# A two-layer graph kernel on one core: tile lists and row ranks moved to the head of the dense stage

## The chip, the cores and the metric

The kernel runs on one core of a Trainium2 chip. The metric is the time on the device in microseconds; the kernel before takes 857.63 us, the median of three runs (855.54 to 860.32). Its profile was taken from one further execution with a span of 857.5 us.

## The reference

There are 8 batches of 2048 nodes with 128 features, and one 2048 x 2048 matrix `adj`, which is sparse: about 0.4% of it is nonzero, and it is weighted.

```python
def layer0(x):                            # relation = adj
    w_j, w_i, w_r = g_w[:128], g_w[128:256], g_w[256]
    res = (x @ w_i)[:, :, None] + (x @ w_j)[:, None, :] + adj[None] * w_r + g_b
    return einsum('bij,bjd->bid', res, x) @ weight + bias

def layer1(x):                            # A1 = A2 = adj
    x1 = einsum('bnf,nw->bwf', x, adj)
    x2 = 2 * einsum('bnf,nw->bwf', x1, adj) - x
    xs = [x, x1, x2, x1, x2]
    return relu(concat(xs) @ Theta1 + bias1)

x = layernorm(x + layer0(x))
x = layernorm(x + layer1(x))
```

Layer 0 is the product of adj (with the weights folded in, y0 = x @ (w_r * weight)) and a term of rank 9, whose rows are in the tile `ub`. Layer 1 is, after some algebra, two hops: two products with the transpose of adj.

## The kernel before, in words

The 2048 nodes are cut into 16 chunks of 128 (NC). A chunk of outputs of layer 0 could be computed as 16 products of a 128 x 128 block of adj (transposed) with a chunk of y0, for all batches, and the kernel does so for three chunks only (ND = 3), those with 0 to 2. For the other 13 it uses the sparsity of adj: for each tile of 32 output columns it has a list of up to 128 rows that have an entry in that tile, gathers those rows of y0 from memory, gathers the matching rows of adj (called R), and multiplies. Rows that don't fit the lists of the 32-column tiles go into lists of the 64-column halves, and then into one list for the chunk of 128. So a chunk has 4 + 2 + 1 = 7 gathers of y0 and 7 of R. The same lists serve all products with adj.

The stages, in order:

1. *Load* (until about 144 us). `mask_rows` and `y_chunk` (lines 297 and 323) load adj and x, transpose them on the PE, find which tiles have entries on DVE, compute y0 into `Y[c]` (all 16 chunks stay in SBUF), and add up the first dense chunk. The transposed adj goes into the table of R, `rr_d[c]`, one for each sparse chunk: its row n holds the 128 entries of adj to chunk c transposed, and then the 128 entries not transposed. `copy_r` (L410) fills the second half from adj, with one DMA of 1 MB per chunk, in 512-byte pieces. The last 9 rows of each table hold the coefficients of the rank-9 term; they come from the small stores at the end of `more_rows` (L589 to L602, DMA at L599).
2. *Dense stage* (the loop at L798, about 144 to 262 us). Three rounds, c = 0 to 2. Round c ends dense chunk c (`rank1` adds the rank-9 term, `finish0` adds x and does the layernorm), and adds up dense chunk c + 1 in 16 steps j of two 128 x 128 x 512 matmuls (L846). Between these steps the list work is written out by hand: this is where the change is.
3. *Sparse stage of layer 0* (about 258 to 440 us). For each of the 13 chunks in the order `seq` (9 to 14, 3 to 8, 15), `listed_rows` multiplies gathered rows (L881), `finish0` and `make_u` end the chunk. The gathered rows of y0 go to nine buffers, `Y[0]` to `Y[8]`, which the dense stage must have read.
4. *Two hops* of layer 1, with gathers from `u_d` and `y_d` (to the end).

The list work of the dense stage has these parts. `tile_ranks` (L482) counts, with a matmul, the rank of each row in its tile, and keeps 8 rows of each row chunk. `tile_lists` (L496) transposes the result on the PE and sorts each piece with MAX8 on DVE. `tile_lists_end` (L627) turns it into the indices of the tile lists. `half_ranks` and `chunk_ranks` (L528, L541) count the ranks of what is left, by `ranks` (L510): a running sum over the 16 row chunks, with one matmul per row chunk that adds its sums to all later ones. `candidates` (L550) transposes the rest, `list_round` (L558) takes the 8 largest of 2048 per list with MAX8 and strikes them out with MATCH_REPLACE, eight times over, and `chunk_lists_end` (L630) makes the last indices.

`gathers` (L696) issues gathers of R from a fixed list of jobs, `sets` (L686): (c, True) are the four tile lists of a chunk, (c, False) its two half lists and the chunk list. They go to four buffers (`stages`); `keep_r` (L668) copies a landed set under a mask to its place, on DVE. With `mm` given, a gather waits for that matmul ("pace"). In the sparse stage `put` issues what is missing for a chunk before it is used. All gathers are issued by GpSimd (POOL), each in turn (L646). Plain loads, copies and stores around here are issued by SyncE (SP), in the order of the program; a queued store that must wait holds all that follow it. The `pt` PSUM tiles have two buffers, so a tile waits for the last but one to be read.

Where the dense matmuls of round c = 1 meet the list work, one line sets the order: the matmul at j = 8 is placed behind the small matmul at the end of the lists.

Of the kernel before, what the change touches and what calls it, by code (L numbers as in the profile page):

```python
# [18 lines left out]
def kernel(  # L19
# [89 lines left out]
    def flat(t):  # L109
        return t.rearrange("p b f -> p (b f)")  # L110
# [299 lines left out]
    def copy_r(n0, n1):  # L410
        for c in seq[n0:n1]:
            tc.keep_in_program_order(
                nc.sync.dma_start(out=rr_d[c - ND][0:N, 1, :], in_=adj[:, c * P:(c + 1) * P])
            )
# [67 lines left out]
    def tile_ranks():  # L482

        for g in range(2):
            pr = p_tr.tile([P, NC // 2, NT], F32, name=f"pr{g}", tag="pt")
            cs = slice(g * NC // 2, (g + 1) * NC // 2)
            tc.keep_in_program_order(
                nc.tensor.matmul(pr, ut, one[:, cs, :], start=True, stop=True)
            )
            nc.vector.scalar_tensor_tensor(  # L490
                onen[:, cs, :], pr, 8.0, onen[:, cs, :], op0=ALU.is_le, op1=ALU.mult
            )
        nc.vector.tensor_add(hit, pairs(onen)[:, :, :, 0], pairs(onen)[:, :, :, 1])
        nc.vector.scalar_tensor_tensor(half, hit, 0.0, half, op0=ALU.is_equal, op1=ALU.mult)
# [14 lines left out]

    def ranks(out, m):  # L510

        tc.keep_in_program_order(
            nc.tensor.matmul(out, lt, m, start=True, stop=False, skip_group_check=True)
        )
        for c in range(NC - 1):
            tc.keep_in_program_order(nc.tensor.matmul(
                out[:, c + 1:, :], ones,
                m[:, c, None, :].to_broadcast([P, NC - 1 - c, m.shape[2]]),
                start=False, stop=(c == NC - 2), skip_group_check=True,
            ))  # L520

    def split(rank, m, mn, lo, hi, most):

# [34 lines left out]
    def list_round(r):  # L558
        top = lists[0:96, 64 + 8 * r:72 + 8 * r]
        part = cand[0:96].rearrange("p c n -> p (c n)")  # L560
        tc.keep_in_program_order(nc.vector.max(top, part))
        if r < 7:
            nc.vector.match_replace(part, top, part, 0.0)
# [6 lines left out]
    def make_ub():  # L570
        lq3 = lq.rearrange("p (b m) -> p b m", b=B)
        cs4 = rows4("cs4")
        for h in range(2):
            nc.scalar.copy(cs4[:, h * HB:(h + 1) * HB, :], pcs[h])
        pcq = p_tr.tile([P, B, 2], F32, name="pcq", tag="pt")
        for b in range(B):
            nc.tensor.matmul(
                pcq[:, b, :], cs4[:, b, :], sel[:, 0:2 + b % HB:1 + b % HB], start=True, stop=True
            )
        nc.vector.tensor_copy(lq[:, 0:(B - 1) * (B + 2) + 1:B + 2], pcq[:, :, 0])  # L580
        nc.vector.tensor_copy(lq3[:, :, B], pcq[:, :, 1])
        for h in range(2):
            pu = p_sm.tile([B + 1, HB, D], F32, name=f"pu{h}", tag="sm")
            for i in range(HB):
                nc.tensor.matmul(pu[:, i, :], lq3[:, h * HB + i, :], w_sb, start=True, stop=False)
                nc.tensor.matmul(pu[:, i, :], e8, b0row, start=False, stop=True)
            nc.vector.tensor_copy(ub[:, h * HB:(h + 1) * HB, :], pu)

    def more_rows():  # L589

        tc.keep_in_program_order(nc.sync.dma_start(out=y0_d[N:, :], in_=flat(ub)))
        n = (NC - ND) * (B + 1)
        ps = p_tr.tile([P, P], F32, name="ps", tag="pt")
        nc.tensor.transpose(ps[0:n, :], si[:, ND:, :].rearrange("p c b -> p (c b)"), ident)
        t = rows4("sit_all")
        nc.vector.memset(t[:, 1, :], 0.0)
        nc.scalar.copy(t[0:n, 0, :], ps[0:n, :])
        for c in seq:
            tc.keep_in_program_order(nc.sync.dma_start(  # L599
                out=rr_d[c - ND][N:, :, :],  # L600
                in_=t[(B + 1) * (c - ND):(B + 1) * (c - ND + 1), 0:2, :],
            ))  # L602
# [24 lines left out]
    def tile_lists_end():  # L627
        return lists_end(0, LP, [(h, 0, lists[:, 0:64], 64 * h, NT) for h in range(2)])
# [167 lines left out]
    with nc.allow_non_contiguous_dma(reason="512-byte rows of blocks"):  # L796
        pending, accs, xr = None, acc0, load_x(0, "xr", nc.sync)
        for c in range(ND):  # L798
            if c + 1 < ND:
                xr1 = load_x(c + 1, "xr", nc.sync)  # L800
            if c == 0:
                copy_r(2, NC - ND)
                tile_ranks()
                make_ub()
                more_rows()
                rank1(0, accs, si_t(0))
            else:
                z = finish0(c, accs, xr, c > 1)
            if c == 1:
                for n in range(NC):  # L810
                    tc.keep_in_program_order(
                        nc.sync.dma_start(out=y0_d[n * P:(n + 1) * P, :], in_=flat(Y[n]))
                    )
            if c + 1 < ND:
                accs1, sit, at1 = acc_pair(), si_t(c + 1), first_at[c + 1]
                for j in range(NC):
                    if c == 0:
                        if j == 0:
                            tile_lists()
                            z = finish0(c, accs, xr, False)  # L820
                        if j == 3:
                            at = tile_lists_end()
                            half_ranks()
                        if j == 6:
                            chunk_ranks()
                        if j in (8, 9):
                            candidates(2 * j - 16)
                            candidates(2 * j - 15)
                        if j == 10 or j == 13:
                            list_round(j // 13)  # L830
                        if j == 11:
                            layernorm(z, "0_0", at)
                    else:
                        if j < 8 and j % 3 < 2:
                            list_round(2 + j // 3 * 2 + j % 3)
                        if j == 8:
                            made, at = chunk_lists_end()
                            layernorm(z, "0_1", at)
                            fetch_own(0, y0_d, seq[0])
                            late0 = fetch_block(0, seq[0])  # L840
                    if (c > 0 or j > 3) and not (c == 1 and j > 12):
                        gathers(3 if c == 1 and j == 12 else 1 if j % 4 == 3 else 2, mm)
                    if c == 1 and j > 12:
                        fetch_lists(0, y0_d, seq[0], 2 * j - 24)
                    for h in range(2):
                        mm = nc.tensor.matmul(  # L846
                            accs1[h], at1[:, j, :], Y[j][:, h * HB:(h + 1) * HB, :],
                            start=(j == 0), stop=False, skip_group_check=True,
                        )
# [228 lines left out]
```

## Time and profile before

| | PE | DVE | ACT | POOL |
|---|---|---|---|---|
| busy us of 857.5 | 757.0 | 363.6 | 173.7 | 427.3 |
| share | 88% | 42% | 20% | 50% |

| costliest groups | count | busy us | mean ns |
|---|---|---|---|
| gathers from y0 and y, POOL L646 | 203 | 201.4 | 992 |
| gathers of R, POOL L646 | 91 | 92.3 | 1014 |
| gathers from u, POOL L646 | 112 | 111.1 | 992 |
| matmuls of listed rows, PE L881, into rc | 896 | 219.8 | 605 |
| matmuls of the dense stage, PE L846 | 128 | 61.5 | 633 |

In all, the DMA engines move 269.19 MB. A line "PE MATMUL acc<-Y,wide 128*128 128x512" is a matmul from tile Y with weights from tile wide; each matmul in float32 leaves two records. DMA_INDIRECT is a gather; "rr_d" is the table of R, "in_adj_dram" the matrix, "y_d" stands for y0_d in stage 3 and for y_d later. Times are from the start of the span. A busy PE is not a PE at its peak, and idle time of an engine off the chain of waits costs nothing.

### The profile page before, as it was taken

The page shows a single profiled execution, that of the slowest core. Times are in us where ns is not written, and L with a number is a line of the kernel's source. Part 1 is how long each engine was busy: PE and PEld are TensorE (multiplying, and loading weights), DVE is VectorE, ACT ScalarE, POOL GpSimd, SP SyncE. Part 2 cuts the span into 40 slices and gives each one's busy share as a digit, 9 for nine tenths or more (in the row PEclk, how much of TensorE's full clock was granted, in tenths as well). Part 3 has the DMA queues.
Part 4 walks back from the last instruction along what each step waited for, and adds up shares of the span by engine and source line. Part 5 has one row for each costly group of instructions (what it writes and reads, how often), then busy time and mean ns, then how long its engine had stood idle before and what let it go on. Part 6 is the DMA issues. An engine that isn't in the chain of part 4 may idle for free.

```text
span 857.5 us, 10765 instructions
## 1 busy us (share of the span) xinstructions
PE 757.0 (88%) x3594; PEld 377.8 (44%) x3594; DVE 363.6 (42%) x1060; ACT 173.7 (20%) x428; POOL 427.3 (50%) x438
## 2 busy tenths in 40 slices
PE   5999999999468898889997998899999999999993
PEld 4666665464134443434344443343433354544441
DVE  5555667344963453535453010000100075665664
ACT  3665664010002121212222000000000011111111
POOL 0000000007767777777764567766565556666660
PEclk9999999699869999999998999999999999999998
DMA  8699998998728999999996899999997899999994
GB/s 288 197 308 309 309 308 237 301 271 341 269 73 297 329 364 340 343 338 378 369 391 213 291 357 357 369 369 371 385 378 273 312 341 356 351 335 337 326 339 136
DMA packets 177548, 269.19 MB, mean 314 GB/s; under 512 B 17698, under 2 KB 127701, under 8 KB 175438
## 3 DMA queue, kind: packets, MB, share of 16 engines
q0 software_dynamic: 50400, 151.21, 48.7%
q1 hardware_dynamic: 103900, 90.02, 32.7%
q10 hardware_dynamic: 23186, 27.20, 8.7%
q8 instruction: 30, 0.49, 0.2%
q14 instruction: 32, 0.26, 0.1%
HBM read 246.75 MB, written 62.55 MB: 361 GB/s over the span
## 4 chain that ended last, share of the span: by engine, by line
DMA 39%; PE 21%; issue 7%; POOL 3%; DVE 1%; POOLq 0%; ACT 0%; DVEq 0%
DMA Y<-y_d,idx 22%; DMA Y<-u_d,idx 15%; PE acc L881 12%; PE acc L865 4%; PE acc L939 3%; POOL Y L646 2%; DMA stage<-rr_d,idx 2%; POOL stage L646 1%; PE pt_p L184 1%; PE pt_r L957 1%; PE pp L402 1%; DMA rd<-in_adj_dram 1%; POOLq L646 0%; DVE st L211 0%; DVE z L229 0%
## 5 line engine op out<-in xcount | busy, mean ns | idle before, releaser
L646 POOL DMA_INDIRECT Y<-y_d,idx x203 | 201.4, 992 | 105.7 <-PE acc L881 53.7
L881 PE MATMUL acc<-Y,rc 128*32 128x512 f32 (+2 forms) x896 | 219.8, 605 | 24.5 <-DMA Y<-u_d,idx 14.3
L646 POOL DMA_INDIRECT stage<-rr_d,idx x91 | 92.3, 1014 | 225.5 <-PE pc L554 190.5
L646 POOL DMA_INDIRECT Y<-u_d,idx x112 | 111.1, 992 | 64.5 <-PE acc L881 35.4
L881 PEld LDWEIGHTS acc<-Y,rc 128*32 128x32 f32 (+2 forms) x896 | 58.6, 128 | 175.4 <-issue 83.7
L881 PE MATMUL acc<-Y,rct 128*32 128x512 f32 (+2 forms) x364 | 108.6, 618 | 17.0 <-DMA Y<-y_d,idx 16.2
L865 PE MATMUL acc<-Y,rd 128*128 128x512 f32 x148 | 70.7, 601 | 4.1 <-DMA rd<-rr_d 4.1
L881 PEld LDWEIGHTS acc<-Y,rct 128*32 128x32 f32 (+2 forms) x364 | 26.3, 128 | 89.3 <-issue 44.4
L846 PE MATMUL acc<-Y,wide 128*128 128x512 f32 x128 | 61.5, 633 | 0.0
L219 ACT ACTIVATE st<-st,epst 128x8 f32<-128x8 f32 x32 | 9.9, 310 | 243.3 <-DVE st L218 243.3
L383 DVE TENSOR_TENSOR xs<-acc,xs 128x512 f32<-128x512 f32 x26 | 17.7, 682 | 93.5 <-PE acc L881 77.7
L176 DVE COPY z<-acc 128x512 f32<-128x512 f32 x9 | 6.2, 692 | 110.2 <-PE acc L881 57.9
L184 PE MATMUL pt_a<-ident,rc 128*128 128x128 f32 x256 | 38.3, 285 | 6.5 <-DMA rc<-in_adj_dram 6.0
L958 DVE TENSOR_TENSOR z<-acc,b1bc 128x512 f32<-128x512 f32 x32 | 21.5, 685 | 42.8 <-PE acc L865 27.6
L332 PE MATMUL acc<-wx,tr_x 128*128 128x130 f32 x256 | 36.5, 286 | 3.5 <-ACT tr_x L178 3.1
L311 DVE TENSOR_REDUCE stage<-rct 128x64 f32<-128x2048 f32 x13 | 29.7, 2286 | 23.0 <-ACT rct L178 23.0
L303 DVE TENSOR_REDUCE rc<-rc 128x64 f32<-128x2048 f32 x16 | 36.5, 2279 | 5.8 <-DMA rc<-in_adj_dram 5.8
L332 PEld LDWEIGHTS acc<-wx,tr_x 128*128 128x128 f32 x256 | 32.8, 194 | 13.8 <-ACT tr_x L178 6.2
L184 PEld LDWEIGHTS pt_a<-ident,rc 128*128 128x128 f32 x256 | 31.4, 147 | 16.3 <-issue 14.8
L342 PE MATMUL acc<-Y,wide 128*128 128x512 f32 x64 | 36.4, 652 | 1.7 <-ACT Y L336 0.9
L846 PEld LDWEIGHTS acc<-Y,wide 128*128 128x128 f32 x128 | 25.0, 203 | 29.0 <-issue 28.1
L959 DVE SCALAR_TENSOR_TENSOR z<-z,pt_r 128x512 f32<-128x512 f32 x32 | 20.5, 682 | 37.9 <-PE pt_r L957 37.9
(216 smaller groups left out, 897.3 us busy)
## 6 DMA issues: line engine op xcount, KB each, us to landing
rc<-in_adj_dram SPq DMA_DIRECT2D x16, 1024.0 KB
rr_d<-rct SPq DMA_DIRECT2D x13, 1024.0 KB
rr_d<-in_adj_dram SPq DMA_DIRECT2D x13, 1024.0 KB
xs<-in_x_dram SPq DMA_DIRECT2D x21, 512.0 KB
y_d<-Y SPq DMA_DIRECT2D x16, 512.0 KB
out_dram<-z ACTq DMA_DIRECT2D x16, 512.0 KB
u_d<-u ACTq DMA_DIRECT2D x15, 512.0 KB
Y<-y_d SPq DMA_DIRECT2D x15, 512.0 KB
```

Source lines behind the costliest of these rows:

```text
L184: mm = nc.tensor.transpose(pt[:, i, :], s, ident)
L303: nc.vector.tensor_reduce(mk[:, c, :], a.rearrange("p (w f) -> p w f", f=TW), AX.X, ALU.max, apply_absolute_value=True,)
L311: nc.vector.tensor_reduce(mkt[:, :, 4 * c:4 * c + 4], at.rearrange("p j (t f) -> p j t f", f=TW), AX.X, ALU.max, apply_absolute_value=True,)
L332: nc.tensor.matmul(py[:, i, 0:D + 2], xt[b // HB][:, (b + i) % HB, :], wx, start=True, stop=True,)
L342: nc.tensor.matmul(acc0[h], first_at[0][:, c, :], Y[c][:, h * HB:(h + 1) * HB, :], start=(c == 0), stop=False, skip_group_check=True,)
L646: g = nc.gpsimd.indirect_dma_start(out=out, out_offset=None, in_=src, in_offset=bass.IndirectOffsetOnAxis(ap=ids[:, n:n + 1], axis=0), bou ...
L846: mm = nc.tensor.matmul(accs1[h], at1[:, j, :], Y[j][:, h * HB:(h + 1) * HB, :], start=(j == 0), stop=False, skip_group_check=True,)
L865: in_order(nc.tensor.matmul(accs[h], r, t[:, h * HB:(h + 1) * HB, :], start=start, stop=stop, skip_group_check=True,))
L881: in_order(nc.tensor.matmul(accs[h][w * t:w * t + w], r[:, o + w * t:o + w * t + w], gs[t][:, h * HB * D:(h + 1) * HB * D], start=False, s ...
L939: in_order(nc.tensor.matmul(accs[h][:, b, :], x1t[c][:, h * HB + b, :], th[:, i, :], start=(b == 0), stop=False, skip_group_check=True,))
L958: nc.vector.tensor_add(z[:, hs, :], accs[h], b1bc.to_broadcast([P, HB, D]))
L959: nc.vector.scalar_tensor_tensor(z[:, hs, :], z[:, hs, :], 0.0, pt, op0=ALU.max, op1=ALU.add)
```

## The change

The list work is moved to the head of the dense stage, and three things go with it.

- *Order.* The tile lists, half ranks and chunk ranks come before round 0's last step, rather than at j = 0, 3 and 6; candidates at j = 0 and 1 rather than 8 and 9; six list rounds in round 0 (at every second step from 5) rather than two; the end of the lists at j = 7 of round 1 rather than 8.
- *Ranks by groups.* `ranks` sums groups of four row chunks on DVE (`four`). Within a group it adds each chunk to the later ones of the group with three matmuls over all groups at once, and then each group's sum to all later groups, with three more. It is seven matmuls for sixteen.
- *Stores.* The small stores for the table of R stand behind two copies of adj (four with the two before them), not behind all; the other nine copies follow them. The store of `ub` to y0_d moves to round 1. In `make_ub` the row b0row is added by one matmul for four batches.
- *Gathers.* Two gathers of R are issued at every step of round 0 from the first on, three at its end, and 23 in round 1: 58 in the dense stage, where it was 47. The list of jobs has all tile lists but the last at its front.

```diff
     def ranks(out, m):
-        tc.keep_in_program_order(
-            nc.tensor.matmul(out, lt, m, start=True, stop=False, skip_group_check=True)
-        )
-        for c in range(NC - 1):
-            tc.keep_in_program_order(nc.tensor.matmul(
-                out[:, c + 1:, :], ones,
-                m[:, c, None, :].to_broadcast([P, NC - 1 - c, m.shape[2]]),
-                start=False, stop=(c == NC - 2), skip_group_check=True,
-            ))
+        w = m.shape[2]
+        four = two.rearrange("p c w -> p (c w)")[:, 0:NG * w].rearrange("p (g w) -> p g w", w=w)
+        o4, m4 = [t.rearrange("p (g k) w -> p g k w", k=4) for t in (out, m)]
+        nc.vector.tensor_reduce(four, m.rearrange("p (g k) w -> p g w k", k=4), AX.X, ALU.add)
+        add(out, lt, m, start=True, stop=False)
+        for k in range(3):
+            add(o4[:, :, k + 1:, :], ones,
+                m4[:, :, k:k + 1, :].to_broadcast([P, NG, 3 - k, w]), start=False, stop=False)
+        for g in range(NG - 1):
+            add(out[:, 4 * g + 4:, :], ones,
+                four[:, g:g + 1, :].to_broadcast([P, NC - 4 - 4 * g, w]),
+                start=False, stop=(g == NG - 2))
...
             pu = p_sm.tile([B + 1, HB, D], F32, name=f"pu{h}", tag="sm")
+            nc.tensor.matmul(
+                pu, e8, b0row[:, None, :].to_broadcast([1, HB, D]), start=True, stop=False,
+                skip_group_check=True,
+            )
             for i in range(HB):
-                nc.tensor.matmul(pu[:, i, :], lq3[:, h * HB + i, :], w_sb, start=True, stop=False)
-                nc.tensor.matmul(pu[:, i, :], e8, b0row, start=False, stop=True)
+                nc.tensor.matmul(
+                    pu[:, i, :], lq3[:, h * HB + i, :], w_sb, start=False, stop=(i == HB - 1),
+                    skip_group_check=True,
+                )
...
     def more_rows():
-        tc.keep_in_program_order(nc.sync.dma_start(out=y0_d[N:, :], in_=flat(ub)))
...
-    sets = [(c, True) for c in seq[:10]]
+    sets = [(c, True) for c in seq[:-1]]
     for n, c in enumerate(seq):
         sets.append((c, False))
-        if n in (0, 4, 7):
-            sets.append((seq[10 + (0, 4, 7).index(n)], True))
+        if n == 4:
+            sets.append((LAST, True))
...
             if c == 0:
-                copy_r(2, NC - ND)
+                copy_r(2, 4)
                 tile_ranks()
+                tile_lists()
+                half_ranks()
                 make_ub()
                 more_rows()
+                copy_r(4, NC - ND)
+                at = tile_lists_end()
+                chunk_ranks()
                 rank1(0, accs, si_t(0))
+                mm = None
             else:
                 z = finish0(c, accs, xr, c > 1)
             if c == 1:
+                tc.keep_in_program_order(nc.sync.dma_start(out=y0_d[N:, :], in_=flat(ub)))
                 for n in range(NC):
...
                     if c == 0:
-                        if j == 0:
-                            tile_lists()
+                        if j < 2:
+                            candidates(2 * j)
+                            candidates(2 * j + 1)
+                        if j == 2:
                             z = finish0(c, accs, xr, False)
-                        if j == 3:
-                            at = tile_lists_end()
-                            half_ranks()
-                        if j == 6:
-                            chunk_ranks()
-                        if j in (8, 9):
-                            candidates(2 * j - 16)
-                            candidates(2 * j - 15)
-                        if j == 10 or j == 13:
-                            list_round(j // 13)
-                        if j == 11:
                             layernorm(z, "0_0", at)
+                        if j > 4 and j % 2:
+                            list_round((j - 5) // 2)
                     else:
-                        if j < 8 and j % 3 < 2:
-                            list_round(2 + j // 3 * 2 + j % 3)
-                        if j == 8:
+                        if j in (1, 3):
+                            list_round((j + 11) // 2)
+                        if j == 7:
                             made, at = chunk_lists_end()
                             layernorm(z, "0_1", at)
                             fetch_own(0, y0_d, seq[0])
                             late0 = fetch_block(0, seq[0])
-                    if (c > 0 or j > 3) and not (c == 1 and j > 12):
-                        gathers(3 if c == 1 and j == 12 else 1 if j % 4 == 3 else 2, mm)
-                    if c == 1 and j > 12:
-                        fetch_lists(0, y0_d, seq[0], 2 * j - 24)
+                    if c == 0:
+                        gathers(2, mm)
+                    elif j < 11:
+                        gathers(3 if j in (7, 8) else 1 if j == 3 else 2, mm)
+                    else:
+                        fetch_lists(0, y0_d, seq[0], 2 * j - 20)
...
-                        if c == 1 and j == 8:
+                        if c == 1 and j == 7:
                             behind(mm, made)
                 rank1(c + 1, accs1, sit)
                 if c == 0:
-                    gathers(2, mm)
+                    gathers(3, mm)
```

More of the change, by code (lines that the diff above doesn't have):

```diff
@@ L510, in ranks, with add @@
     def ranks(out, m):
-        tc.keep_in_program_order(
-            nc.tensor.matmul(out, lt, m, start=True, stop=False, skip_group_check=True)
-        )
-        for c in range(NC - 1):
-            tc.keep_in_program_order(nc.tensor.matmul(
-                out[:, c + 1:, :], ones,
-                m[:, c, None, :].to_broadcast([P, NC - 1 - c, m.shape[2]]),
-                start=False, stop=(c == NC - 2), skip_group_check=True,
-            ))
+        def add(o, wt, mv, **flags):
+            tc.keep_in_program_order(
+                nc.tensor.matmul(o, wt, mv, skip_group_check=True, **flags)
+            )
[11 more added lines that the diff above has]
+                start=False, stop=(g == NG - 2))
     def split(rank, m, mn, lo, hi, most):
@@ L583, in make_ub @@
             pu = p_sm.tile([B + 1, HB, D], F32, name=f"pu{h}", tag="sm")
+            nc.tensor.matmul(
+                pu, e8, b0row[:, None, :].to_broadcast([1, HB, D]), start=True, stop=False,
+                skip_group_check=True,
+            )
             for i in range(HB):
[L585 to L586 removed]
+                nc.tensor.matmul(
+                    pu[:, i, :], lq3[:, h * HB + i, :], w_sb, start=False, stop=(i == HB - 1),
+                    skip_group_check=True,
+                )
             nc.vector.tensor_copy(ub[:, h * HB:(h + 1) * HB, :], pu)
     def more_rows():
[L591 removed]
         n = (NC - ND) * (B + 1)
```

## The prediction

> **What bounds the kernel now.** I read the chain of waits first, then the page's slices, then the busy times by stage, and last the timeline around the one stage that the change touches. The chain that ended last is mostly transfers:
>
> ```profile
> DMA 39%; PE 21%; issue 7%; POOL 3%; DVE 1%; POOLq 0%; ACT 0%; DVEq 0%
> ```
>
> Its first piece lies at 233 us and is a gather of R; from there it runs through gathers to the end. So the end is set by when gathers start and how fast they pass. The busy times by stage (columns: stretch, its length, busy us of PE, weight load, DVE, ACT, POOL with counts, granted clock, DMA share, GB/s) show where they do not pass at full rate:
>
> ```profile
> 144.00:190.00 46.00, 45.98 (x195) 25.07 (x192) 21.90 (x61) 4.18 (x9) 0.00 (x0) 0.85 1.06 296
> 190.00:200.00 10.00, 10.00 (x49) 6.38 (x48) 3.94 (x3) 2.33 (x4) 5.92 (x6) 1.00 0.56 175
> 200.00:220.00 20.00, 20.00 (x48) 8.51 (x47) 11.51 (x15) 0.26 (x1) 15.21 (x16) 1.00 1.03 414
> 223.00:243.00 20.00, 0.25 (x1) 0.00 (x0) 19.79 (x18) 0.00 (x0) 15.43 (x16) 0.64 0.47 146
> 243.00:258.00 15.00, 14.88 (x37) 6.80 (x38) 6.08 (x35) 1.57 (x4) 8.26 (x9) 0.80 0.22 60
> 258.00:440.00 182.00, 162.38 (x712) 72.36 (x711) 82.12 (x333) 39.20 (x87) 134.42 (x135) 0.98 0.97 348
> ```
>
> From 144 to 190 the PE and the DMA are full, but POOL does nothing. From 223 to 243 the PE does nothing, with DVE full. From 223 to 258 the DMA runs at 0.47 and then 0.22: 20 x 0.53 + 15 x 0.78 = 22 us of transfer time unused; from 190 to 200 another 4.4. In the sparse stage of layer 0 (258 to 440) DMA (0.97), PE (162 of 182) and POOL (135 gathers at a pitch of 1.30 us, 175 of 182) are all nearly full. The timeline tells why:
>
> ```profile
> 147.95 37.80 SPq L413 DMA_DIRECT2D rr_d<-in_adj_dram  x11
> 172.68 6.90 PE L516 MATMUL rank_h<-wide,ones 128*128 128x480 f32 x30
> 184.22 4.13 PE L516 MATMUL rank_c<-wide,ones 128*128 128x240 f32 x30
> 185.85 1.97 SPq L591 DMA_DIRECT2D y_d<-ub  x1
> 187.93 7.07 SPq L599 DMA_DIRECT2D rr_d<-sit_all  x13
> 192.56 1.16 POOL L646 DMA_INDIRECT stage<-rr_d,idx  x1 [190.47 <-PE pc L554]
> 195.54 21.72 SPq L812 DMA_DIRECT2D y_d<-Y  x16
> 240.69 2.29 DVE L561 MAX8 rc<-wide 96x8 f32<-96x2048 f32 x1
> 243.12 0.61 PE L608 MATMUL pl<-ident,rc 96*64 96x32 f32 x8 [19.87 <-DVE rc L561]
> 247.86 1.00 POOL L646 DMA_INDIRECT stage<-rr_d,idx  x1 [4.61 <-PE acc L846]
> 258.96 1.00 POOL L646 DMA_INDIRECT Y<-y_d,idx  x1 [0.31 <-issue]
> ```
>
> The tile lists are ready at 173, but the first gather starts at 192.56: its table needs the small stores, issued at 187.93 behind eleven copies. (PE pc, which the wait names, is only the last semaphore seen; the same store lies 4.6 us before.) From 192.56 POOL runs at its pitch, 47 gathers of R and one pause of 4.6 us, to the first gather of y0 at 258.96. The PE waits there for the eighth list round on DVE. Only two rounds had run when the sums of 215 to 216 were done; the other six, 4.6 us each with a mask between, followed back to back until 243.
>
> **What the skill says.** "DMA: Bandwidth & Descriptors", section "Issuing engines are not separate DMA queues": transfers of all issuing engines run on the same 16 engines and interleave. The trace agrees: from 200 to 220 stores and gathers share them at 1.03. So early gathers of R slow the copies and stores beside them. The same page, "Anatomy of one DMA — SWDGE (gpsimd) path", puts the fixed part of a transfer that GpSimd issues at about 2 us, most of it the write's receipt. The small stores are SyncE's, and here one took up to 4.6 us from issue to its first reader, with copies ahead of it; I use the 4.6. "TensorE: Matmul & The Clock Gate", Part 1: idle time of about 3.4 us or more halves the clock. The trace shows 0.50 in the idle stretch from 230 to 240, and 0.50 from 160 to 170, where the PE worked on small operands.
>
> **The change part by part.**
> *Ranks by groups.* Half ranks stream 512 + 32 x 120 = 4352 columns now and 512 + 384 + 256 + 128 + 384 + 256 + 128 = 2048 after. They took 171.72 to 179.41, 7.7 us, so 3.6 remain. Chunk ranks fall from 2176 to 1024 columns: 4.4 us (183.79 to 188.20) to 2.1. PE saves 6.4 us. Two DVE reductions come in, unseen in this shape: 512 elements cost between 0.57 (a quarter of the 2.28 us row of L303) and 1.1 us (the strided L548, 0.57 for 256). I take 1.0 and 0.5; behind them only the last three matmuls of each rank wait, so they are hidden.
> *Row of ub.* Thirty-two records took 5.95 us (153.17 to 159.12, part at half clock). Sixteen remain (8 x 0.32) and four of 512 columns come in (4 x 0.43): 4.2 us. It saves about 1.5 us of PE.
> *Lists and stores at the head.* Masks are done at 147.3. Then tile ranks (to 150.1 on DVE), 32 transposes and 8 MAX8 (2 us on PE at full clock, 1.8 on DVE: 154), half ranks and split (3.6 + 4.5: about 160), and the transpose for the small stores, which shares two PSUM buffers with these, at about 159; its copy takes 0.3. Where it adds a wait: behind the small stores SyncE holds nine copies and then all y0 stores. Two copies (7 us) fill its queue until 155, so it idles about 5 us. First store about 160, landing 4 to 5 us later; indices (7 small DVE operations, after the ub products) about 165. I put the first gather at 167 (162 to 174), 25 us earlier.
> *Gathers at every step.* 58 instead of 47 run in the dense stage. Without pauses they take 58 x 1.30 = 75 us: POOL comes to y0 at 242. It no longer waits for the PE, which needs 1.72 us per step against 2.6 for two gathers.
> *DMA up to there.* From 144 to 223 before, 79 us less 4.4 idle less 24 gathers x 0.42 (7.7 gathers in 10 us make a share of 0.32) leave 64.5 us of other transfers. With 58 x 0.42 = 24 it makes 89, and with the bubble of 5 the y0 stores are down at 144 + 94 = 238. That too is just under 242: nothing in this window has slack.
> *List rounds.* They may start at about 176: the head's PE work with the rank-one product, which ended at 165.1 before, takes in lists and ranks (2 + 3.6 + 2.1 less the 1.5 of ub) and so ends near 170, and the sums (2 x 0.69) and the first layernorm (173.19 to 177.65 before, 4.5) follow. The rounds need 8 x 2.29 + 7 x 2.36 = 35 us, eight masks 4, the next sums 1.4: 217. The PE, 223.2 - 6.4 - 1.5 - 1.7 (the wait moved up one step), is there at about 214. The 20 us of PE idleness become about 3. Then nine steps, 15.5, the rank-one product, 2, and 2 more if the clock halves in the wait: about 237, below POOL's 242.
> *Sum for this stage.* First gather of y0 at 243 instead of 259: 16 us.
> *Sparse stage.* Eleven gathers of R leave it. On POOL they are worth 14.3 us, on the DMA 11 x 0.42 = 4.6. With DMA at 0.97 the DMA value counts: 5 us. The hops after it are untouched (0 us).
> Total 16 + 5 = 21: 857.6 - 21 = 836.6, say 836.
>
> **Rivals.**
> *All overlap gained.* The DMA closes all 26 us of unused time and POOL's relief shows too: first gather at 162, y0 at 238, and 9 us from the sparse stage. 30 us off: 828. For it: POOL at 175 of 182. Against: PE and DMA are as full there.
> *Stores of y0 late.* The R gathers take DMA share from copies and y0 stores, or the bubble on SyncE is 15 us, and y0 starts at 252. Then 7 us there and, as DMA stays the bound, 3 of the 5 in the sparse stage: 847 or 848. I put it at 847. For it: my two ends lie 4 us apart, and the copies' 512-byte pieces are slow (290 GB/s).
> *Slower.* The chain at the head runs at half clock and the small stores stop SyncE: transpose at 175 (20 us bubble), and each of 13 stores waits for the one before (2 us each, 26). Then y0 stores end at 144 + 89 + 46 = 279, 20 us later than the first gather of y0 now; less the 5 of the sparse stage, 872 or 873. I put it at 872. For it: SyncE works its queue in order. Against: the 13 stores took 7.07 us together before.
>
> **How the numbers follow.** The forecast has 0.6, all overlap 0.15, late stores 0.18, slower 0.07. The range reaches from 822 (all overlap, with POOL's full 14.3 us in the sparse stage: 857.6 - 21 - 14.3) to 853 (y0 at 254 and nothing gained after: 857.6 - 5). It leaves out the slower case and the tails of the others. Faster by over 0.5% (below 853.3) 0.9, within 0.5% 0.04, slower 0.06.
>
> **What would show it.** First gather of R near 167; ranks 3.6 and 2.1 us; PE idle before the last list transposes under 6 us rather than 19.9; DMA share near 1.0 from 165 to 240; first gather of y0 near 243; hop lengths as before. It is wrong if small stores leave late, if y0 stores are still running when POOL reaches y0, or if the sparse stage takes as long as before.

## The result and the profile after

The changed kernel takes 827.27 us (median of 4 runs, 825.16 to 832.94) beside 856.59 us for the kernel before: a ratio of 0.9652, with a 95% interval of 0.9599 to 0.9706. Run again later beside other kernels it was at 0.9688 (0.9641 to 0.9736). So it is about 3 to 3.5% faster, 26 to 29 us between the medians. I had forecast 836 us, which is 21 us, with a range of 822 to 853.

In the changed kernel the tile lists and both ranks stand ahead of the rank-one product of round 0, and so ahead of all 16 steps of its loop. The chain of waits of the kernel after ends like the one of before, in transfers, but it now goes back through DVE and PE to the start of the kernel. Before, it could be followed only to a gather of R at 233 us, so the shares of the two chains cannot be compared one by one.

```profile
PE 41%; DMA 40%; issue 8%; DVE 4%; ACT 3%; POOL 2%; POOLq 0%; SPq 0%; DVEq 0%; ACTq 0%
```

Busy times by stage (columns as for before: stretch, length, busy us and counts of PE, weight load, DVE, ACT, POOL, granted clock, DMA share, GB/s):

```profile
144.00:166.00 22.00, 22.00 (x115) 12.10 (x112) 16.28 (x36) 1.10 (x3) 0.00 (x0) 1.00 0.74 214
166.00:190.00 24.00, 24.00 (x90) 13.11 (x89) 20.49 (x42) 5.47 (x11) 18.37 (x19) 1.00 1.02 316
190.00:207.00 17.00, 17.00 (x41) 7.13 (x40) 16.97 (x20) 0.26 (x1) 13.04 (x14) 1.00 1.12 362
207.00:217.00 10.00, 1.14 (x7) 0.34 (x7) 7.97 (x10) 0.00 (x0) 7.87 (x8) 0.78 1.03 419
217.00:242.00 25.00, 24.58 (x82) 12.34 (x80) 12.16 (x58) 3.45 (x8) 19.21 (x20) 0.88 0.82 316
242.00:440.00 198.00, 169.36 (x761) 76.30 (x760) 89.22 (x358) 43.60 (x98) 134.12 (x135) 0.97 0.96 349
```

The DMA is full from 166 to 217, and the long stretches of before at 0.47 and 0.22, just ahead of the first gather of y0, have no counterpart of that length. POOL is busy at its full pitch from 166 to 254. The PE has one idle stretch of 9 us, from 208 to 217, in place of 20. What is left unused lies in two places: 0.74 from 144 to 166 (0.15 from 157 to 168), and 0.82 from 217 to 242 (0.44 from 233 on). The last row has 135 gathers like the last row of before, but ten of them are gathers of adj for the next stage, which came behind 440 before. The timeline has the same events as before, and two new lines at its end:

```profile
147.77 4.73 SPq L413 DMA_DIRECT2D rr_d<-in_adj_dram  x2
154.93 1.46 PE L514 MATMUL rank_h<-wide,ones 128*128 128x384 f32 x6
161.63 4.66 SPq L612 DMA_DIRECT2D rr_d<-sit_all  x13
166.33 31.43 SPq L413 DMA_DIRECT2D rr_d<-in_adj_dram  x9
166.14 1.18 POOL L659 DMA_INDIRECT stage<-rr_d,idx  x1 [164.06 <-DMA rr_d<-sit_all]
216.80 0.61 PE L621 MATMUL pl<-ident,rc 96*64 96x32 f32 x8 [8.86 <-DVE rc L569]
242.34 1.00 POOL L659 DMA_INDIRECT Y<-y_d,idx  x1 [0.31 <-ACT st L219]
250.85 1.04 PE L896 MATMUL acc<-Y,rct 128*32 128x512 f32 x2 [1.69 <-DMA Y<-y_d,idx]
259.87 0.99 POOL L659 DMA_INDIRECT Y<-y_d,idx  x1 [6.17 <-PE acc L896]
```

The small stores go out at 161.63, the first gather of R starts at 166.14 and the first of y0 at 242.34. POOL had no pause between these two. At 254 POOL has filled all nine buffers for y0 and waits 6.17 us for the PE to free the first. The PE in turn waits for the gathered rows to land: 1.69 us ahead of the first listed rows at 250.85, and 1.75 and 0.77 us more by 256.

Cut at three events, the two traces compare so (us; "changed, again" is the second trace of the same kernel):

| stretch | before | changed | changed, again |
|---|---|---|---|
| start to the first gather of R | 192.6 | 166.1 | 166.5 |
| to the first gather of y0 | 66.4 (47 gathers) | 76.2 (58) | 76.5 (58) |
| to the first gather of u (sparse stage) | 206.0 | 197.7 | 196.9 |
| to the end (hops) | 392.6 | 391.1 | 387.0 |
| span | 857.5 | 831.2 | 826.9 |

So of 26 to 31 us, 16 to 17 come from the earlier start of y0 and 8 to 9 from the sparse stage. The hops, which the change doesn't touch, differ by 4 us between two traces of one kernel, and that much of any single comparison can be scatter.

### The profile page after: what moved, and what is told of

Same layout as the page of the kernel before. It is cut to its first block, busy times and chain, and to the rows that moved or that the text cites. A ratio compares the mean times of both kernels' runs of the same rounds, so it can differ in the third digit from the quotient of the medians.

```text
span 831.2 us, 10667 instructions
## 1 busy us (share of the span) xinstructions
PE 740.9 (89%) x3546; PEld 370.0 (45%) x3546; DVE 365.0 (44%) x1062; ACT 173.3 (21%) x428; POOL 426.8 (51%) x438
## 4 chain that ended last, share of the span: by engine, by line
PE 41%; DMA 40%; issue 8%; DVE 4%; ACT 3%; POOL 2%; POOLq 0%; SPq 0%; DVEq 0%; ACTq 0%
DMA Y<-y_d,idx 20%; DMA Y<-u_d,idx 13%; PE acc L896 12%; PE acc L880 5%; PE acc L342 4%; PE acc L332 4%; PE acc L954 4%; DMA stage<-rr_d,idx 4%; PE acc L861 3%; PE pt_a L184 2%; POOL Y L659 2%; DVE rc L569 2%; DMA rc<-in_adj_dram 1%; PE pt_x L184 1%; PE pp L402 1%
## 5 line engine op out<-in xcount | busy, mean ns | idle before, releaser
L896 PE MATMUL acc<-Y,rct 128*32 128x512 f32 (+2 forms) x364 | 105.7, 628 | 22.9 <-DMA Y<-y_d,idx 22.4
```

Of the source, the lines that this page charges most:

```text
L896: in_order(nc.tensor.matmul(accs[h][w * t:w * t + w], r[:, o + w * t:o + w * t + w], gs[t][:, h * HB * D:(h + 1) * HB * D], start=False, s ...
```

## The experiments

My theory was that the start of the stream of gathers on POOL sets when the sparse stage begins, and the small stores set that start. The rivals were that the saving came from the PE's idle time before the list rounds alone, or from the number of gathers placed early.

### The small stores alone, on the kernel before

```diff
-                copy_r(2, NC - ND)
+                copy_r(2, 4)
                 tile_ranks()
                 make_ub()
                 more_rows()          # its store of ub moves to round 1
+                copy_r(4, NC - ND)
```

> The kernel before with one edit: the small stores for the table of R stand behind two copies of adj, the other nine copies follow, and the store of ub moves to round 1. Lists and gathers stay where they were. The prediction said that these stores alone held the first gather at 192.6 us. If so, the first gather comes at about 175 to 180 us, and the 47 gathers are done earlier, but the PE still waits for list rounds until 243: 845 to 855. Rival: the first gathers also wait for the matmuls of step 3 (the pace), which ran at 189 to 192 us; then the first gather stays at 189 to 192 and the time at 855 to 860.

Measured: 845.61 us, a ratio of 0.9888 (0.9836 to 0.994). The timeline of this kernel, POOL's lines and the PE's wait for the lists, with the idle time and its releaser in brackets:

```profile
172.16 1.16 POOL L645 DMA_INDIRECT stage<-rr_d,idx  x1 [170.07 <-DVE rct L621]
179.27 1.00 POOL L645 DMA_INDIRECT stage<-rr_d,idx  x1 [4.65 <-PE acc L847]
188.91 0.99 POOL L645 DMA_INDIRECT stage<-rr_d,idx  x1 [3.42 <-PE acc L847]
235.27 0.62 PE L607 MATMUL pl<-ident,rc 96*64 96x32 f32 x8 [13.54 <-DVE rc L561]
240.01 1.00 POOL L645 DMA_INDIRECT stage<-rr_d,idx  x1 [7.47 <-PE acc L847]
251.12 1.00 POOL L645 DMA_INDIRECT Y<-y_d,idx  x1 [0.30 <-issue]
```

The first gather moves from 192.56 to 172.16, as soon as the indices are there. This settles what the wait named "PE pc" was: the stores. But the gathers then pause for the matmuls that pace them: 4.65 and 3.42 us, and 7.47 us behind the list rounds, where it was 4.61 before. The rival about the pace was wrong on the first gather and right on the third and later ones. So of 20.4 us at the first gather, 7.8 reach the first gather of y0. I had also expected the PE to wait for list rounds until 243. It waits until 235.27, though no list round was moved; the next experiment shows why. The stores alone are about a third of the saving (by the interval, 0.6 to 1.6% of 3 to 3.5%).

### The small stores late, on the changed kernel

```diff
-                copy_r(2, 4)
+                copy_r(2, NC - ND)
...
                 more_rows()
-                copy_r(4, NC - ND)
```

> The changed kernel with one part undone: the small stores follow all copies of adj. Theory (the start of the gathers sets the end of the dense stage): first gather at about 190 instead of 166, 58 gathers at 1.30 us, first gather of y0 at about 266 instead of 242, and a time of 845 to 853. Rival (what was gained is the idle time of the PE and the better filled transfers, whenever the gathers start): list rounds still start at 176, time 827 to 835.

Measured: 852.32 us, 0.997 of the kernel before (0.9948 to 0.9992). Nearly all is lost with this one edit undone.

```profile
192.81 1.16 POOL L659 DMA_INDIRECT stage<-rr_d,idx  x1 [190.73 <-DMA rr_d<-sit_all]
203.58 0.29 DVE L687 TENSOR_TENSOR rct<-stage,has 128x128 f32<-128x128 f32 x1 [22.74 <-issue]
239.76 0.61 PE L621 MATMUL pl<-ident,rc 96*64 96x32 f32 x8 [31.93 <-DVE rc L569]
269.17 0.99 POOL L659 DMA_INDIRECT Y<-y_d,idx  x1 [0.30 <-issue]
```

The first gather is back at 192.81, and 58 gathers later, at 269.17, y0 begins: 10 us later than in the kernel before. The sparse stage is then 194.8 us, 11 shorter than before. The PE waits 31.93 us for the lists, more than in any other run. The list rounds stand between masks of gathered tiles on DVE. The first list round is over at 180.84; the first mask, ahead of the second round, runs only at 203.58, when the first gathered tiles are there, and DVE stands for 22.74 us (the view names no releaser for this wait; the order of the program and the gathers' start at 192.81 do). So late gathers make late lists, and in the run before this one earlier gathers made earlier lists. This is more than I had expected: the stores hold both chains, not only POOL's. Early stores are needed for the rest to pay. Alone they give about a third.

### The list rounds late

```diff
-                        if j > 4 and j % 2:
-                            list_round((j - 5) // 2)
+                        if j == 10 or j == 13:
+                            list_round(j // 13)
...
-                        if j in (1, 3):
-                            list_round((j + 11) // 2)
+                        if j < 8 and j % 3 < 2:
+                            list_round(2 + j // 3 * 2 + j % 3)
```

> The changed kernel with two list rounds in round 0 and six in round 1, as before, and all else early. The rounds then end at about 228 instead of 217 and the PE waits about 20 us instead of 9. Theory (POOL's stream of gathers bounds, the PE has 2 to 3 us to spare): the first gather of R stays at 166, that of y0 at 242 to 245, the PE is 8 to 11 us later at the first listed rows, and the time rises by 5 to 9 us, to 832 to 837. Rival (PE idle time before the lists costs nothing while POOL is full): within 2 us of 827.

Measured: 836.68 us, 0.9772 (0.9723 to 0.982), 9.4 and 7.6 us above the two medians of the changed kernel (827.27 and 829.05).

```profile
230.93 0.61 PE L621 MATMUL pl<-ident,rc 96*64 96x32 f32 x8 [22.60 <-DVE rc L569]
233.42 1.00 POOL L659 DMA_INDIRECT stage<-rr_d,idx  x1 [4.23 <-issue]
247.38 0.99 POOL L659 DMA_INDIRECT Y<-y_d,idx  x1 [0.30 <-issue]
```

The first gather of R stays at 166.53. The PE now waits 22.60 us and reaches the first listed rows at 264.33 instead of 250.85. POOL stops as well, for 4.23 us, as the gathers of the half lists need the last indices, which DVE makes after the PE's transposes at 230.93 and has written by 232.68. So the list rounds are a second chain beside the start of the gathers, and it reaches POOL and the PE alike. The time rose by about what I had expected. But POOL was not full here, so the rival, that idle time of the PE costs nothing while POOL is full, is not tested by itself. The first gather of y0 comes 5.0 us later, and later than the 242 to 245 that I had put, and the tenth, the first that needs a buffer back, 6.6 us later (266.50 for 259.87). So most of the loss goes through POOL, and some 2 us are left for the PE, which reads the first listed rows without a wait here.

### 47 gathers of R in the dense stage

The eleven others go back to the sparse stage.

```diff
-    sets = [(c, True) for c in seq[:-1]]
+    sets = [(c, True) for c in seq[:11]]
...
-                        gathers(3 if j in (7, 8) else 1 if j == 3 else 2, mm)
+                        gathers((2, 2, 2, 1, 2, 0, 0, 3)[j] if j < 8 else 0, mm)
```

> The changed kernel with 47 instead of 58 gathers of R in the dense stage; the other eleven go into the sparse stage, as in the kernel before. Theory of the prediction (each of the eleven costs the sparse stage 0.42 to 1.3 us of transfer or POOL time, and the dense stage does not start y0 earlier, as its stores are not down): 832 to 840. Rival (the stream of gathers on POOL is one sum, and only where it pauses matters): the first gather of y0 comes at about 228, 14 us earlier, the sparse stage takes 14 us longer, the 6 us pause of POOL at 253 to 260 is filled by gathers of R, and the time is 821 to 828.

Measured: 832.46 us, 0.9725 (0.9669 to 0.9781). The interval overlaps that of the changed kernel, so the times alone don't tell the two apart. The trace does:

```profile
226.86 1.00 POOL L659 DMA_INDIRECT stage<-rr_d,idx  x1 [0.30 <-issue]
235.69 0.99 POOL L659 DMA_INDIRECT Y<-y_d,idx  x1 [7.83 <-DMA rd<-rr_d]
```

POOL is done with R at 228 and then stands for 7.83 us. SyncE issued the sixteen y0 stores from 204.74 to 224.58, so the last is issued 11 us before the first gather that reads the table. The wait ends by a DMA (the one named was issued right behind the stores, and the gather doesn't read it), and no buffer or index was missing; by elimination it is the y0 stores, which as I had put it are not down sooner. y0 gains 6.7 us and the sparse stage loses 8.0 (205.7 against 197.7): 0.73 us for each of the eleven gathers, between its 0.42 of DMA time and its 1.30 on POOL. As the sparse stage took 194.8 to 199.0 us in ten traces with 58 gathers, this is only good to 0.6 to 1.0. The rival fell: y0 does not begin at 228, the pause at 253 to 260 is gone as it said, and the time does not fall for it.

### The ranks by sixteen matmuls

`ranks` of the kernel before in the changed kernel.

> The changed kernel with ranks counted by sixteen matmuls, as before. Theory (the ranks stand ahead of the transpose for the small stores and of the list rounds): half ranks take 7.5 us instead of 3.5, so the first gather comes at about 170, y0 at about 246; chunk ranks add 2.3, the list rounds start near 182 and end near 223, and the time rises by 4 to 6 us above the changed kernel. Rival (matmuls of the dense sum fill the PE there, so the ranks cost nothing): within 2 us of the changed kernel.

Measured: 832.32 us, 0.9728 (0.9684 to 0.9772), beside the changed kernel run on the same chip at 829.05, 0.9688 (0.9641 to 0.9736):

> The changed kernel itself, once more, beside the next three on one chip: 0.960 to 0.971 of the kernel before, first gather of R at 166, first gather of y0 at 242.

```profile
154.68 6.90 PE L516 MATMUL rank_h<-wide,ones 128*128 128x480 f32 x30
168.85 1.16 POOL L651 DMA_INDIRECT stage<-rr_d,idx  x1 [166.77 <-PE pu L589]
245.66 1.00 POOL L651 DMA_INDIRECT Y<-y_d,idx  x1 [0.30 <-issue]
```

The half ranks, without the first matmul of each sum, cost 6.90 us where they take 2.9 by groups. The first gather comes 2.4 us later than in the changed kernel beside it (166.47), y0 2.7 later (243.00). So a part of the 4 us reaches the gathers. In time the medians differ by 3.3 us, and the intervals overlap: the direction is what I expected, the size a little below it, and the time alone doesn't show it.

### Stores and indices earlier still

In the changed kernel SyncE waited 9 us for the transpose behind the half ranks, with the DMA at 0.74. Three kernels take that away step by step. The first moves stores and indices:

```diff
                 copy_r(2, 4)
+                more_rows()
+                copy_r(4, NC - ND)
                 tile_ranks()
                 tile_lists()
+                at = tile_lists_end()
                 half_ranks()
                 make_ub()
-                more_rows()
-                copy_r(4, NC - ND)
-                at = tile_lists_end()
                 chunk_ranks()
```

> The changed kernel with the transpose and the small stores ahead of all list work, and the end of the tile lists right behind the MAX8, ahead of the half ranks. First gather of R at 157 to 159 instead of 166, no gap in SyncE's queue at 152 to 161, y0 at 233 to 235. Theory (two chains end nearly together, POOL's stream and the list rounds with the PE behind them): the list rounds still end at 217, so the PE reaches the listed rows as late as now, and only 0 to 4 us are gained. Rival (POOL's stream alone bounds): 7 to 9 us are gained.

Measured: 826.12 us, 0.9656 (0.9615 to 0.9698), 2.9 us under the changed kernel beside it, with overlapping intervals. The first gather comes at 161.68, 4.5 us earlier, and y0 begins at 238.54, 3.8 us earlier; both are later than I had put them, as the stores, issued from 154.03 on, hold the first gather still. The time is within the theory's 0 to 4 us and not the rival's 7 to 9. The second also moves the layernorm of dense chunk 0 behind the end of the lists, and starts the rounds two steps sooner:

```diff
-                            layernorm(z, "0_0", at)
-                        if j > 4 and j % 2:
-                            list_round((j - 5) // 2)
+                        if j > 2 and j % 2:
+                            list_round((j - 3) // 2)
...
+                            layernorm(pending[1], "0_0", at)
                             layernorm(z, "0_1", at)
```

> As the one before, and the layernorm of dense chunk 0 moves behind the end of the lists, so that the list rounds start right after the candidates, at every second step from 3. Theory of two chains: the rounds start at about 171 and end at about 211, the PE waits 3 to 4 us instead of 9, the first listed rows come 5 us earlier, and with POOL's stream 8 us earlier the time falls by 5 to 8 us below the changed kernel. Rival (POOL's stream or the y0 stores alone bound): no more than the one before.

Measured: 825.2 us, 0.9651 (0.9611 to 0.969). It was run once more:

> The kernel with early stores, early indices and the moved layernorm once more, beside the one without the pace: 0.961 to 0.969 of the kernel before, first gather of R at 160, y0 at 240, PE wait before the lists 5 us.

Measured: 824.98 us, 0.9645 (0.9614 to 0.9675). POOL and PE of the kernel with both edits, first trace:

```profile
160.19 1.19 POOL L659 DMA_INDIRECT stage<-rr_d,idx  x1 [158.11 <-DMA rr_d<-sit_all]
212.43 0.62 PE L621 MATMUL pl<-ident,rc 96*64 96x32 f32 x8 [5.05 <-DVE rc L569]
240.11 1.00 POOL L659 DMA_INDIRECT Y<-y_d,idx  x1 [0.30 <-issue]
```

The first gather starts 6 us earlier than in the changed kernel and the PE waits 5.05 us rather than 8.86, but y0 begins only 2.2 us sooner, as POOL now pauses for the pace (1.53 us at 175, 2.54 at 185). I had expected 5 to 8 us of time; the medians are 2 to 4 us lower than the two of the changed kernel, and no interval separates them. The third kernel puts the small stores ahead of all eleven copies, since the indices were ready at 156 and the stores not:

> As the kernel with the moved layernorm, but the small stores stand ahead of all eleven remaining copies instead of behind two. There the indices were ready at 156 and the first gather started only at 160, and the DMA share fell to 0.59 from 155 to 166 while SyncE worked through the small stores. Theory (early stores and full transfers still limit): first gather at 156 to 157, DMA share above 0.9 from 155 to 166, first gather of y0 at 232 to 235, time 3 to 6 us below the one with the moved layernorm, at 0.958 to 0.962 of the kernel before. Rival (the PE with the list rounds, or the landing of the y0 stores, bounds by now): first gather earlier, but the first listed rows and the time as there, 0.964 to 0.967.

Measured: 826.41 us, 0.9664 (0.9622 to 0.9705).

```profile
156.94 1.16 POOL L659 DMA_INDIRECT stage<-rr_d,idx  x1 [154.85 <-DVE idr L638]
175.16 0.99 POOL L659 DMA_INDIRECT stage<-rr_d,idx  x1 [4.80 <-PE acc L860]
240.60 1.00 POOL L659 DMA_INDIRECT Y<-y_d,idx  x1 [0.31 <-issue]
```

The stores hold nothing any more: the first gather comes with the indices, at 156.94, 9.2 us before that of the changed kernel. But the gathers of round 0 are paced by the matmuls of the step before, and those wait for the head's own work on the PE. POOL pauses 4.80 us at 175 and 2.54 at 185. y0 begins at 240.60, where it was at 240.11. My theory of 232 to 235 and 3 to 6 us fell, and the time is the rival's.

### The gathers without the pace

The gathers of round 0 lose their tie to the matmuls.

```diff
                     if c == 0:
-                        gathers(2, mm)
+                        gathers(2)
...
-                    gathers(3, mm)
+                    gathers(3)
```

> As the one with the small stores first, and the gathers of round 0 no longer wait for a matmul of the step before (their buffers and tables still order them). There the first gather came at 157 but POOL paused 4.8 us at 175 and 2.5 us at 185 for that matmul, and y0 began at 240.6 as with the later start. Theory (the pace took the place of the stores as the wait): no such pauses, first gather of y0 at 232 to 236, time 3 to 7 us below, at 0.957 to 0.962 of the kernel before. Rival (the PE behind the list rounds, which reaches the listed rows at 247 there, or the landing of the y0 stores bounds): y0 gathers start earlier or wait for their stores, and the time stays at 0.963 to 0.968.

Measured: 864.44 us beside 884.01 for the kernel before, a ratio of 0.9771 (0.974 to 0.9801). The kernel before took 849 to 864 in all other comparisons. Why both took longer here is not known, and I draw nothing from it. Once more:

> The kernel without the pace in round 0 once more, as its first execution fell where the kernel before took 884 us too and engines waited for things outside the kernel. Theory (the pace took the place of the stores as the wait): POOL fills its four buffers by 178, is then held to one set per list round (5 us, against 5.2 for four gathers), pauses 3 us or less, first gather of y0 at 233 to 238, time at 0.957 to 0.963 of the kernel before. Rival (the four buffers, which come free behind the list rounds on DVE, hold the gathers as much as the pace did): pauses of 5 to 8 us in all, y0 at 238 to 241, 0.963 to 0.968.

Measured: 823.84 us, 0.9652 (0.9616 to 0.9688).

```profile
184.30 0.99 POOL L659 DMA_INDIRECT stage<-rr_d,idx  x1 [6.56 <-DVE rc L687]
239.24 1.00 POOL L659 DMA_INDIRECT Y<-y_d,idx  x1 [0.30 <-issue]
```

The rival held. The four buffers of gathered tiles take the place of the pace: they come free by masks on DVE, which stand between the list rounds, and POOL waits 6.56 us for one. y0 begins at 239.24. Three waits in a row (stores, pace, buffers) have been taken away or uncovered, 9.6 us at the first gather became 3.1 at y0, and the time is not separated from the changed kernel's.

The traces show a fourth wait behind these. In the five traces of these last kernels (leaving out that of the 864 us run) y0 begins between 238.54 and 240.60, but its tenth gather, the first that needs a buffer back, comes at 255.7 to 256.0 in all five, some 4 us ahead of the changed kernel's. From there to the first gather of u it takes 179.3 to 180.3 us, in these five and in the five other traces with 58 gathers, those with late stores, late rounds and old ranks included. So in these traces what lies ahead of the sparse stage counts only through the moment at which the first of the nine buffers comes free. In the five traces the PE stands ready there and waits for gathered rows to land, and the 2 us between their starts of y0 make no difference. Which transfers hold these rows was not tested.

So the lowest median of these, 823.84, and the four others from 825.0 to 826.4 are at most a few us below the changed kernel. I don't call any of them faster.

## Why the prediction was right, and where its sizes were off

- *Direction and mechanism.* They held: the small stores hold the start of the gathers, and without early stores the rest gives almost nothing. Two opposite experiments show it (0.9888 with the stores alone, 0.997 with all but the stores). The stores are not enough, though: alone, they move the first gather by 20.4 us and y0 by 7.8, as the gathers then pause. The saving was 26 to 29 us rather than 21; the time lies in the range. It lies nearer to the 828 of the rival *All overlap gained* than to my 836. That rival had the 9 us of the sparse stage right and the dense stage wrong (162 and 238, where 166.1 and 242.3 were measured).
- *First gather at 167, first gather of y0 at 243.* Measured 166.14 and 242.34. Fifty-eight gathers took 76.2 us for the 75 that I had from the pitch of 1.30 us. DMA share from 165 to 240, put near 1.0: 0.97.
- *Ranks of 3.6 and 2.1 us.* Measured 3.4 (154.07 to 157.52) and 2.0 (165.26 to 167.28). The reductions took 1.02 and 0.57 us, where I had put 1.0 and 0.5. Without the groups the first gather comes 2.4 us later, for the 4.1 that the half ranks save in my sum. The row of ub took 3.8 us (1.88 from 144.36 and 1.92 from 163.41) for 4.2.
- *SyncE's gap of 5 us.* It was 9.0 us, and the DMA share from 144 to 166 only 0.74. I had the transpose at 159 and it came at 161.03, behind the half ranks and four dense matmul records (my terms for ranks and split, 154 + 3.6 + 4.5, make 162 and not 160); and I counted two copies as work until 155, while they were issued by 152.5. The term was too small by 4 us, but it was not the last to end: y0 waited for POOL, not for its stores.
- *y0 stores down at 238.* In the kernel with 47 gathers, where they are waited for, the first reader starts at 235.69. The last y0 store was issued 11 us before it was waited out. This fits what I took from the Trainium skill, "DMA: Bandwidth & Descriptors", section "Issuing engines are not separate DMA queues", that gathers, copies and stores share the same engines: in the changed kernel they have a share of 1.03 to 1.12 together from 190 to 217. When the stores land in the changed kernel itself no line shows.
- *PE waiting under 6 us for the lists.* It waited 8.86. The lists came when I had said (216.8 for 217), the PE earlier (208 for 214). I had carried over the clock of before, which stood at 0.50 from 157 to 168; in the changed kernel it was 1.00 from 144 to 207. Eleven us at half the clock are worth 5.5 us, an estimate from these two figures, and 6 were missing. The Trainium skill, "TensorE: Matmul & The Clock Gate", Part 1, ties the clock to how busy the PE has been; the PE counts as busy in both traces there, so busy time by the profile doesn't tell which clock is granted. Why it fell before is not shown. That the estimate of the lists came out right is luck in part. It took over the half clock for the head's PE work (its terms, 165.1 + 6.2, make 171 and not 170), and it left out that the list rounds wait on DVE for masks of gathered tiles, which the late stores showed; this cost little only because the gathers came when they did. The 8.86 us themselves are not shown to cost anything: the PE waits again, for gathered rows, at 250.85.
- *Sparse stage shorter by 5 us.* Here the sum was mis-sized: it was 8.2 and 9.1. I took eleven gathers at their DMA time of 0.42 us, because the DMA was at 0.97. The experiment with 47 gathers gives 0.73 each (0.6 to 1.0), 8.0 us in all. So in this stage, where DMA, POOL and PE are all nearly full, the work that was taken out was worth a value between its times on the two.
- *The hops at 0 us.* They were 1.5 and 5.6 us shorter in the two traces; the two traces of one kernel differ by 4.1. In ten other traces (all but that of the 864 us run) they took 386 to 390, so the one trace of before is the longest. What of this is scatter and what is real stays open.

## What to carry to other kernels

A stage that is full on three engines can still be shifted as a whole: look for the earliest wait ahead of it, here a few stores of 9 KB queued behind 11 MB of copies, rather than for work inside it. Undo each edit alone, in both directions, before sharing out a gain: the stores gave a third alone, and without them the other edits gave almost nothing. And when a wait is removed, name the next one that will hold the same instruction; here the pace of the matmuls and then the free buffers took back 3.7 of 6.0, 7.5 of 9.2 and 6.5 of 9.6 us. Then ask whether the stage is set there at all: here it was set later, when the first buffers came free.

## What the runs showed that I had not expected

- The granted clock at the head of the dense stage (157 to 168) was 0.50 in the kernel before and 0.56 in the same kernel with early stores. In all twelve traces of the changed kernel and its variants it was 1.00. The PE counted as busy throughout in all of them. The DMA share there was 1.11 and 0.69 where the clock was low and 0.15 to 1.11 where it was full, and the ranks by sixteen matmuls left it full, so neither the transfers' load nor the ranks explain it. What only the two kernels with the low clock have is the row of ub by eight pairs of small matmuls and the old order of the matmuls around it. Which of these does it was not tested.
- A store that SyncE issues at the end of a queue of 8 MB, with gathers beside it, was waited for until 11 us after its issue, and the small stores of 9 KB with copies ahead until 4.5 to 7.7 us after theirs (161.63 to 166.14, and 154.03 to 161.68 in the kernel with stores and indices moved; counted from the first of the thirteen).
- Late gathers made the lists late: with late stores the PE waited 31.93 us for list rounds that need nothing from the gathers. They only share DVE's order with the masks that do.
